# First tokens and weights in pieces, the first norm in halves, and idle matmuls ahead of the first product

## The chip, the cores and the metric

The kernel runs on one core of one Trainium2 chip. The metric is device time in microseconds (us) from one execution of the program; lower is better. Five engines work side by side, each with its own in-order instruction stream: TensorE (PE in the profile, with PEld for its weight loads), VectorE (DVE), ScalarE (ACT), GpSimd (POOL) and SyncE (SP), which issues all of this kernel's DMAs.

## The reference

There are 4 sequences of 1024 tokens with 1024 channels, all in float32. With `xn` the layernorm of the tokens over channels (no scale, no shift):

```
xn   = (x - mean) / sqrt(var + 1e-5)
ug   = xn * sigmoid(xn @ gate_w.T + gate_b)
aa   = tanh(a); um = mean over tokens of ug
d_eff = d + um @ d_lr_u @ d_lr_v / 4
s    = G * cumsum(b * ug / G),  G = cumprod(aa)       # per channel, over tokens
s    = c * s + d_eff * ug
h    = silu(silu(xn @ w1.T) @ w3.T) @ w2.T            # all tokens
top-2 routing: softmax(xn @ wr.T) -> expert numbers 0..7 and two gates
out_moe[expert number] += gate * h                    # rows 0..7 of the flat token axis alone
result = x + s * silu(out_moe)
```

An expert number is used as a row number, so only the first 8 rows of the result differ from `x`. All other work feeds those 8 rows: every token goes through the products with `w1` and `w3`, and every token of the first sequence through the gate product as well. Only the first 8 rows need `s`, so the recurrence is short.

## The kernel before

**Tiling.** Tokens are worked in four superblocks of 1024. The three big products are called `u` (tokens by `w1`), `g` (tokens by `gate_w`, superblock 0 alone) and `m` (the result of `u` by `w3`). Each is one Strassen-Winograd level over 2 x 2 blocks (seven block products instead of eight, names 1 to 7), and a block product is again divided into seven or, where it is called plain, eight small products. One small product is `small`, four `matmul` calls of 128x256 with two passes each, which makes the groups of eight matmuls that the profile shows. Operands are tokens with channels on the partitions (`xn[sb, I, J]`, token half I, channel half J) and weight blocks; sums and differences of blocks are made by DVE and POOL (`left_sums`, `t_sum`, `sub`).

**Order.** The order of the whole program is written out by hand. `at(place, f)` puts a piece of work at a place, a number on a scale in which one small product step of a block product is 2; `run_todo` runs what is due before each step. Every engine call goes through `Pinned`, which keeps the program order on each engine, and makes nearly every row of the profile carry line 89, so rows are told apart by tile names. `u` block 1 has steps at places 0, 2, 4, ... 14, and `g` block 1 at places 3, 5, ... 17. Both are plain, and both use the first token block `xn[0, 0, 0]`, with weight blocks `w1` (0, 0) and `gate_w` (0, 0). `u` block 2 starts at 16, `g` block 2 at 19 and `u` block 5 at 31. SP issues its DMAs in the same order; at most eight of them are outstanding in the head of the program.

**The head.** For superblock 0 the statistics are taken of tokens on the partitions. `load_x0` brings 256 tokens as two DMAs of 512 KB. `stats0` then does, on DVE, `bn_stats` twice for each 128 tokens (512 channels each) and a `bn_aggr`; it adds EPS, and ACT takes the square root; `scales` makes the reciprocal square root with one Newton step; four `tensor_scalar` calls turn the two means and the two scales into diagonal matrices (`dg`), and two `matmul` calls by a matrix of ones spread them over all partitions, in the PSUM tile `bc_00` (`acc` for the second 256 tokens, `bc_10` and `bc_11` for the others). `norm0` subtracts the mean and multiplies by the scale, on DVE, in place in the token block, each over 128 x 1024 elements. The transposed tokens `xT` come by DMAs of their own; the first block comes in two halves, the first half before and the second after the first weights.

**Weights.** `first_weights` loads the blocks of `w1` and of `gate_w`, each of 1 MB, and makes the Strassen sums from them. Those of `w1` are also written to DRAM for the other superblocks: `kept_sums_1` makes four sums of block 1 on POOL, and `keep_quarter` writes each of them back. POOL also makes the sums that the products need at once (`fresh_sums`, `left_sums`, and `five`, which is four subtractions for block 5).

Lines that matter here: `load_x0` 1007, `stats0` 236, `scales` 219, `norm0` 282, `first_weights` 508, `kept_sums_1` 524, the list of first loads and places 1031 to 1058.

Of the kernel before, what the change touches and what calls it, by code (L numbers as in the profile page):

```python
# [22 lines left out]
def kernel(  # L23
# [44 lines left out]
    NTOK, D = x.shape  # L68
# [6 lines left out]
    NT = SB // P  # L75
    EPS = 1e-5
    HB = ((0, 0), (0, 1), (1, 0), (1, 1))

    class Pinned:
# [27 lines left out]
    ps_sm = ctx.enter_context(tc.tile_pool(name="ps_sm", bufs=1, space=bass.MemoryType.PSUM))  # L107
# [3 lines left out]
    class Held:  # L111
# [11 lines left out]
                self.home.append(self.tile)  # L123

    NB, NQ = 20, 18
    blocks = deque(
        const.tile([P, 4, 2 * Q], F32, tag=f"b{i}", name=f"b{i}") for i in range(NB)
    )
# [4 lines left out]
    def block(uses=1):  # L133
        return Held(blocks, uses)

    def quarter(uses=1):
        return Held(quarters, uses)


    ident = const.tile([P, P], F32, tag="ident", name="ident")  # L140
    make_identity(nc, ident)
    ones = const.tile([P, P], F32, tag="ones", name="ones")
    pool.memset(ones, 1.0)

    sel = const.tile([P, E], F32, tag="sel", name="sel")

# [26 lines left out]
    def at(place, f, *args):  # L173

        seq[0] += 1
        heapq.heappush(todo, (place, seq[0], f, args))
# [25 lines left out]
    start = {}  # L202
# [13 lines left out]
        sync.dma_start(t.tile, xT[sb, I, J])  # L216
        xn[sb, I, J] = t

    def scales(v, w):

        sd = sp.tile([P, w], F32, tag=f"sd{w}", name="sd")
        act.activation(sd, v, AF.Sqrt)
        r0 = sp.tile([P, w], F32, tag=f"r{w}", name="r0")
        dve.reciprocal(r0, sd)
        e = sp.tile([P, w], F32, tag=f"e{w}", name="e")
        dve.tensor_mul(e, r0, r0)
        dve.tensor_mul(e, e, v)
        dve.tensor_scalar(e, e, -0.5, 1.5, ALU.mult, ALU.add)
        return r0, e

    def part(t, a):
        return t[:, 2 * a : 2 * a + 2, :].rearrange("p b (k n) -> p (b k) n", n=Q)
# [3 lines left out]
    def stats0(I, a, xb, lag):  # L236

        mv = sp.tile([P, 2, 2], F32, tag="mv", name=f"mv_{I}{a}")
        for tt in range(2):
            xt = xb[:, 2 * tt : 2 * tt + 2, :]  # L240
            bn = sp.tile([P, 2, nc.vector.BN_STATS_DIM], F32, tag=f"bn{tt}", name=f"bn_{I}{a}{tt}")
            for n in range(2):
                dve.bn_stats(bn[:, n, :], xt[:, n, :])
            dve.bn_aggr(mv[:, tt, :], bn)
        xb.drop()
        v = sp.tile([P, 2], F32, tag="v2", name=f"v_{I}{a}")
        dve.tensor_scalar(v, mv[:, :, 1], EPS, None, ALU.add)
        mean = mv[:, :, 0]
        dg = quarter()
        r0, e = scales(v, 2)  # L250
        dve.tensor_mul(e, e, r0)
        for s, w in ((0, mean), (1, e)):
            for tt in range(2):
                dve.tensor_scalar(
                    dg[:, (2 * s + tt) * P : (2 * s + tt + 1) * P],
                    ident,
                    w[:, tt : tt + 1],
                    None,
                    ALU.mult,
                )  # L260
        if (I, a) == (1, 1):
            bc = ps_sm.tile([P, 2, Q], F32, tag="sm", name="bc_11")
        elif (I, a) == (1, 0):
            bc = ps_y.tile([P, 2, Q], F32, tag="Y", name="bc_10")
        elif a == 1:
            bc = acc.rearrange("p (s n) -> p s n", s=2)
        else:
            bc = ps_acc.tile([P, 2, Q], F32, tag="rows", name="bc_00")
        yield lag
        for s in range(2):  # L270
            pe.matmul(
                bc[:, s, :],
                ones,
                dg[:, s * Q : (s + 1) * Q],
                start=True,
                stop=True,
                skip_group_check=True,
            )
        dg.drop()
        bc0[I, a] = bc  # L280

    def norm0(I, a, J):
        p = part(xn[0, I, J], a)
        bc = bc0[I, a]
        dve.tensor_tensor(p, p, bc[:, 0:1, :].to_broadcast([P, 4, Q]), ALU.subtract)
        dve.tensor_tensor(p, p, bc[:, 1:2, :].to_broadcast([P, 4, Q]), ALU.mult)

    def stats(sb, bcs):


        sums = sp.tile([P, NT], F32, tag="sums", name=f"sums_{sb}")
        sq = sp.tile([P, NT], F32, tag="sq", name=f"sq_{sb}")
        st = sp.tile([P, 2, NT], F32, tag="st", name=f"st_{sb}")
        for n in range(NT // 2):
            xb = block()
            row = sb * SB + n * 2 * P
            sync.dma_start(
                xb.tile.rearrange("p (t h) d -> p t (h d)", t=2),
                x[row : row + 2 * P, :].rearrange("(t p) d -> p t d", p=P),
            )  # L300
            at(here[0] + 5, squares, xb, 2 * n, sums, sq, st)
            yield 9 if sb == 1 else 6
        yield 9
        v = sp.tile([P, NT], F32, tag="v8", name=f"v_{sb}")
        dve.tensor_scalar(v, sq, 1.0 / D, EPS, ALU.mult, ALU.add)
        r0, e = scales(v, NT)
        dve.tensor_mul(st[:, 1, :], r0, e)
        ts = ps_sm.tile([2 * NT, P], F32, tag="sm", name=f"ts_{sb}")
        yield 5
        pe.transpose(ts, st.rearrange("p s t -> p (s t)"), ident)  # L310
        stT = sp.tile([2 * NT, P], F32, tag="stT", name=f"stT_{sb}")
        yield 1
        dve.tensor_copy(stT, ts)
        flat = dramp.tile([2 * NT, P], F32, tag=f"flat_{sb}", name=f"flat_{sb}")
        yield 0.5
        sync.dma_start(flat, stT)
        bcs[sb] = flat
# [124 lines left out]
    weights = {"w1": w1, "gw": gw, "w3": w3}  # L442
# [4 lines left out]
    T_OF = ((1, 0, None), (3, None, 0), (3, 1, None), (2, None, 1))  # L447
    T_AT = (1, 2, 4, 6)

    def load_w(name, KN, uses):  # L450
        t = block(uses)
        sync.dma_start(t.tile, weights[name][KN])
        return t

    def t_sum(o, t, s, j):
# [49 lines left out]
        sync.dma_start(o.tile, kept[{"u": "w1", "m": "w3"}[kind], i, j])  # L505
        op_ts[kind, sb, i, j] = o

    def first_weights(kind, name):

        keep = name == "w1"  # L510

        def S(i):
            return start[kind, 0, i]

        b = {}

        def load(key, KN, uses):
            b[key] = load_w(name, KN, uses)

        def one():  # L520

# [2 lines left out]
        def kept_sums_1():  # L524
            s = []
            for j in range(4):
                o = quarter(1 + (j < 2))
                t_sum(o, b[1], s, j)
                s.append(o)
                if j == 1:  # L530
                    s[0].drop()
                if j == 3:
                    s[1].drop()
                at(S(1) + 12 + 3 * j, keep_quarter, name, 1, j, o)
                yield 3
            b[1].drop()

# [33 lines left out]
            op_t[kind, 0, 3] = b[3]  # L571

        off = 0 if kind == "u" else 1
        load(1, (0, 0), 2 + keep)
        one()
        if keep:
            at(S(1) + 2, kept_sums_1)
        at(-20 + off, lambda: load(2, (1, 0), 2))
        at(-19, two)
        at(-12 + off, lambda: load(5, (0, 1), 3 + keep))  # L580
# [423 lines left out]

    x0 = {}

    def load_x0(I, a):
        xb = block()
        row = I * H + a * 2 * P
        for t in range(2):  # L1010
            sync.dma_start(
                xb[:, 2 * t : 2 * t + 2, :].rearrange("p h d -> p (h d)"),
                x[row + t * P : row + (t + 1) * P, :],
            )
        x0[I, a] = xb

# [11 lines left out]
    USES = {(0, 0): 4, (0, 1): 3, (1, 0): 3, (1, 1): 3}  # L1028
    G = {(0, 0): 2, (0, 1): 2, (1, 0): 1, (1, 1): 2}

    load_x0(0, 0)
    first = block(USES[0, 0] + G[0, 0])
    xn[0, 0, 0] = first
    sync.dma_start(first[:, 0:2, :], xT[0, 0, 0, :, 0:2, :])
    first_weights("u", "w1")
    load_x0(0, 1)
    sync.dma_start(first[:, 2:4, :], xT[0, 0, 0, :, 2:4, :])
    first_weights("g", "gw")
    at(-27, load_x0, 1, 0)
    at(-26, load_x0, 1, 1)  # L1040
    at(-25, load_xn, 0, 0, 1, USES[0, 1] + G[0, 1])
    at(-16, load_xn, 0, 1, 0, USES[1, 0] + G[1, 0])
    at(-15, load_xn, 0, 1, 1, USES[1, 1] + G[1, 1])
    at(-10, lambda: stats0(0, 0, x0[0, 0], 0))
    at(-9, norm0, 0, 0, 0)
    at(-8, lambda: stats0(0, 1, x0[0, 1], 11))
    at(-7, lambda: stats0(1, 0, x0[1, 0], 13))
    at(3.5, norm0, 0, 1, 0)
    at(3.6, lambda: stats0(1, 1, x0[1, 1], 6))
    at(4, norm0, 0, 0, 1)  # L1050
    at(5, norm0, 0, 1, 1)
    at(8, norm0, 1, 0, 0)
    at(9, norm0, 1, 0, 1)
    at(11, norm0, 1, 1, 0)
    at(12, norm0, 1, 1, 1)
    at(26, consts)
    for IJ in HB:
        at(0, lambda IJ=IJ: left.__setitem__(("u", 0, IJ), xn[(0,) + IJ]))
# [2 lines left out]
    for kind, sb, i, plain in line:  # L1061
        h = Half(kind, sb, i, plain)
        halves.append(h)
        S = start[kind, sb, i]
        n = 2 if sb == 0 and kind == "u" and i not in PLAIN_G else 1
# [13 lines left out]
    for sb in range(NS):  # L1079
        n = 2 if sb == 0 else 1  # L1080
# [78 lines left out]
    for n in range(2):  # L1159
        for k in range(2):  # L1160
            for g in range(4):
# [5 lines left out]
                    start=(k == 0),  # L1167
                    stop=(k == 1),
# [85 lines left out]
```

## Time and profile before

| what | value |
|---|---|
| time, median of 3 runs | 851.77 us (849.03 to 855.65) |
| the profiled execution's own time | 850.42 us |
| its span, first to last instruction | 848.7 us |
| mean granted TensorE clock | 0.997 |
| PE busy | 826.4 us, 97% of the span |
| DVE busy / POOL busy / ACT busy | 557.8 / 495.9 / 234.0 us |
| DMA moved | 189.71 MB |
| before 14.12 us: PE busy, DMA engines busy | 2.05 us, 88% |
| 14.12 to 834 us: PE busy | 815.4 of 819.9 us |
| 834 us to the end | 14.7 us, PE busy 9.0 |

In a row of the timeline the first number is the start in us from the first instruction, the second the time from the start of the group to its end; then engine, line, operation, output tile `<-` input tiles, shape and count. In brackets stands how long the engine had been idle before, and what ended the wait. Tiles `b` are the 20 blocks of 1 MB, `q` the 18 quarters of 256 KB; `b<-in_x` is a load of tokens, `b<-in_xT` of transposed tokens, `b<-in_w` of `w1` or `w3`, `b<-in_gw` of the gate weights. `X_u`, `Z_u`, `Y_u` are the PSUM tiles of the products with `w1`, `X_g` and `Z_g` those of the gate.

### The profile page before, as it was taken

The page shows a single profiled execution, that of the slowest core. Times are in us where ns is not written, and L with a number is a line of the kernel's source. Part 1 is how long each engine was busy: PE and PEld are TensorE (multiplying, and loading weights), DVE is VectorE, ACT ScalarE, POOL GpSimd, SP SyncE. Part 2 cuts the span into 40 slices and gives each one's busy share as a digit, 9 for nine tenths or more (in the row PEclk, how much of TensorE's full clock was granted, in tenths as well). Part 3 has the DMA queues.
Part 4 walks back from the last instruction along what each step waited for, and adds up shares of the span by engine and source line. Part 5 has one row for each costly group of instructions (what it writes and reads, how often), then busy time and mean ns, then how long its engine had stood idle before and what let it go on. Part 6 is the DMA issues. An engine that isn't in the chain of part 4 may idle for free.

```text
span 848.7 us, 11126 instructions
## 1 busy us (share of the span) xinstructions
PE 826.4 (97%) x4071; PEld 698.9 (82%) x4071; DVE 557.8 (66%) x894; ACT 234.0 (28%) x374; POOL 495.9 (58%) x374
## 2 busy tenths in 40 slices
PE   4999999989999999999999999999999999999997
PEld 3887888878888868888888778888888688888882
DVE  6959797987699425576797225775993246546642
ACT  0112213676121207343012226531122021220121
POOL 1479999994728764446865753753449444465400
PEclk9999999999999999999999999999999999999998
DMA  9944437721886876629867756649775455555600
GB/s 359 420 170 138 162 159 268 265 111 63 333 324 223 289 269 249 222 87 353 354 215 259 264 183 270 235 164 398 295 246 179 168 190 209 196 190 216 241 1 2
DMA packets 53181, 189.71 MB, mean 224 GB/s; under 512 B 6076, under 2 KB 9324, under 8 KB 41352
## 3 DMA queue, kind: packets, MB, share of 16 engines
q1 hardware_dynamic: 53128, 189.01, 60.5%
q8 instruction: 33, 0.54, 0.3%
q14 instruction: 20, 0.16, 0.1%
HBM read 165.86 MB, written 39.87 MB: 242 GB/s over the span
## 4 chain that ended last, share of the span: by engine, by line
PE 93%; DVE 5%; DMA 0%; issue 0%; ACT 0%; DVEq 0%; ACTq 0%
PE X_u L89 23%; PE X_m L89 22%; PE Z_m L89 12%; PE Z_u L89 11%; PE Y_u L89 5%; PE X_g L89 5%; PE Y_m L89 5%; DVE b L89 4%; PE Z_g L89 3%; PE acc L89 2%; PE plT L89 2%; PE Y_g L89 1%; PE pp L1163 1%; DMA b<-in_x 0%; PE bc L89 0%
## 5 line engine op out<-in xcount | busy, mean ns | idle before, releaser
L89 POOL TENSOR_TENSOR q<-b 128x512 f32<-128x512 f32 x144 | 202.2, 1416 | 231.2 <-DVE b L89 75.9
L89 ACT ACTIVATE b<-b 128x512 f32<-128x512 f32 (+1 forms) x152 | 105.0, 696 | 327.8 <-DVE b L89 318.8
L89 DVE TENSOR_TENSOR b<-b,b 128x512 f32<-128x512 f32 x176 | 177.8, 1030 | 3.0
L89 POOL TENSOR_TENSOR q<-b,q 128x512 f32<-128x512 f32 x91 | 133.1, 1465 | 5.7 <-issue 3.2
L89 POOL TENSOR_TENSOR b<-b,b 128x512 f32<-128x512 f32 x72 | 94.2, 1336 | 40.6 <-PE X_u L89 34.4
L89 DVE TENSOR_TENSOR b<-X_u,b 128x512 f32<-128x512 f32 x87 | 59.9, 689 | 75.5 <-PE X_u L89 74.7
L89 PE MATMUL X_u<-q,q 128*128 128x256 f32 x432 | 103.1, 382 | 1.0 <-DVE b L89 1.0
L89 PE MATMUL X_m<-q,q 128*128 128x256 f32 x416 | 98.3, 379 | 0.0
L89 DVE TENSOR_TENSOR b<-X_m,b 128x512 f32<-128x512 f32 x84 | 57.2, 686 | 62.0 <-PE X_m L89 60.7
L89 PEld LDWEIGHTS X_u<-q,q 128*128 128x128 f32 x432 | 81.3, 190 | 15.9 <-issue 2.6
L89 POOL TENSOR_TENSOR q<-q,b 128x512 f32<-128x512 f32 x53 | 72.0, 1359 | 30.3 <-PE X_u L89 26.2
L89 PEld LDWEIGHTS X_m<-q,q 128*128 128x128 f32 x416 | 79.1, 190 | 10.6
L89 DVE TENSOR_TENSOR b<-b,bc 128x1024 f32<-128x1024 f32 x60 | 72.5, 1212 | 4.3 <-ACT bc L89 2.3
L89 PE MATMUL X_u<-b,b 128*128 128x256 f32 x248 | 60.2, 388 | 5.2 <-DVE b L89 4.9
L89 PE MATMUL X_m<-b,b 128*128 128x256 f32 x272 | 63.8, 381 | 0.4 <-DVE b L89 0.4
L89 PEld LDWEIGHTS X_u<-b,b 128*128 128x128 f32 x248 | 48.0, 195 | 13.3 <-DVE b L89 6.1
L89 PEld LDWEIGHTS X_m<-b,b 128*128 128x128 f32 x272 | 51.5, 190 | 8.2 <-DVE b L89 1.4
L89 DVE TENSOR_TENSOR b<-Z_u,b 128x512 f32<-128x512 f32 x47 | 32.4, 688 | 31.3 <-PE Z_u L89 30.6
L89 PE MATMUL X_u<-b,q 128*128 128x256 f32 x216 | 51.4, 381 | 0.0
L89 PE MATMUL Z_u<-q,b 128*128 128x256 f32 x216 | 51.4, 381 | 0.0
L89 PE MATMUL Y_u<-b,b 128*128 128x256 f32 x216 | 51.3, 381 | 0.0
L89 PE MATMUL Z_u<-q,q 128*128 128x256 f32 x216 | 51.0, 379 | 0.0
(139 smaller groups left out, 1137.8 us busy)
## 6 DMA issues: line engine op xcount, KB each, us to landing
q<-w SPq DMA_DIRECT2D x160, 256.0 KB, 3.7
b<-in_w SPq DMA_DIRECT2D x36, 1024.0 KB, 7.7
b<-w_T SPq DMA_DIRECT2D x24, 1024.0 KB, 5.2
b<-in_xT SPq DMA_DIRECT2D x15, 1024.0 KB, 9.9
w<-q SPq DMA_DIRECT2D x56, 256.0 KB, 5.5
b<-in_x SPq DMA_DIRECT2D x12, 1024.0 KB, 7.3
w_T<-b SPq DMA_DIRECT2D x8, 1024.0 KB, 4.5
b<-in_gw SPq DMA_DIRECT2D x7, 1024.0 KB, 11.4
```

Source lines behind the costliest of these rows:

```text
L89: r = f(*args, **kwargs)
L1163: nc.tensor.matmul(pp[n][g * CG : (g + 1) * CG, :], accT[:, kk, :], w2_sb[n, kk // 4][:, kk % 4, :], start=(k == 0), stop=(k == 1),)
```

## The change

1. Sixteen `matmul` calls of ones by the identity, into a PSUM tile that nobody reads, stand first in PE's stream. A square root of one column stands first in ACT's.
2. The first 256 tokens come as four DMAs of 256 KB. The first half of the first transposed block comes as two DMAs of 256 KB, and the first block of `w1` as two of 512 KB (sub-blocks 0 and 2, then 1 and 3), taken in turns. The first gate weights now stand ahead of the second half of the first transposed block in SP's order.
3. In `stats0` ACT takes the square root straight from the variance, with EPS as its bias. The diagonals of the means are made ahead of the reciprocal, and after the reciprocal the Newton step takes three instructions, the last product folded in (it was four).
4. `norm0` of the first 256 tokens works in two channel halves: subtract and multiply the first, then the second.
5. Places move: the spreading of the second 256 tokens from 3 to 4.5 (after one more `u` step), of the third from 6 to 7, of the fourth from 9.6 to 12.2; the norms of superblock 0 to later places; `kept_sums_1` from 2 to 8 and its writes by 6.

```diff
     NB, NQ = 20, 18
+    IDLE = 16
...
+    eps = const.tile([P, 1], F32, tag="eps", name="eps")
+    pool.memset(eps, EPS)
+
+    root = const.tile([P, 1], F32, tag="root", name="root")
+    act.activation(root, eps, AF.Sqrt)
...
-    def scales(v, w):
-
-        sd = sp.tile([P, w], F32, tag=f"sd{w}", name="sd")
-        act.activation(sd, v, AF.Sqrt)
+    def scales(o, v, sd, w):
+
         r0 = sp.tile([P, w], F32, tag=f"r{w}", name="r0")
         dve.reciprocal(r0, sd)
         e = sp.tile([P, w], F32, tag=f"e{w}", name="e")
-        dve.tensor_mul(e, r0, r0)
+        dve.scalar_tensor_tensor(e, r0, -0.5, r0, ALU.mult, ALU.mult)
         dve.tensor_mul(e, e, v)
-        dve.tensor_scalar(e, e, -0.5, 1.5, ALU.mult, ALU.add)
-        return r0, e
+        dve.scalar_tensor_tensor(o, e, 1.5, r0, ALU.add, ALU.mult)
...
-        v = sp.tile([P, 2], F32, tag="v2", name=f"v_{I}{a}")
-        dve.tensor_scalar(v, mv[:, :, 1], EPS, None, ALU.add)
-        mean = mv[:, :, 0]
+        sd = sp.tile([P, 2], F32, tag="sd2", name=f"sd_{I}{a}")
+        act.activation(sd, mv[:, :, 1], AF.Sqrt, bias=eps)
         dg = quarter()
-        r0, e = scales(v, 2)
-        dve.tensor_mul(e, e, r0)
-        for s, w in ((0, mean), (1, e)):
+
+        def diagonals(s, w):
             for tt in range(2):
...
+        diagonals(0, mv[:, :, 0])
+        v = sp.tile([P, 2], F32, tag="v2", name=f"v_{I}{a}")
+        dve.tensor_scalar(v, mv[:, :, 1], EPS, None, ALU.add)
+        rs = sp.tile([P, 2], F32, tag="rs", name=f"rs_{I}{a}")
+        scales(rs, v, sd, 2)
+        diagonals(1, rs)
...
-    def norm0(I, a, J):
+    def norm0(I, a, J, parts=1):
         p = part(xn[0, I, J], a)
         bc = bc0[I, a]
-        dve.tensor_tensor(p, p, bc[:, 0:1, :].to_broadcast([P, 4, Q]), ALU.subtract)
-        dve.tensor_tensor(p, p, bc[:, 1:2, :].to_broadcast([P, 4, Q]), ALU.mult)
+        w = 4 // parts
+        for h in range(0, 4, w):
+            for s, op in ((0, ALU.subtract), (1, ALU.mult)):
+                row = bc[:, s : s + 1, :].to_broadcast([P, w, Q])
+                dve.tensor_tensor(p[:, h : h + w, :], p[:, h : h + w, :], row, op)
...
-    def load_w(name, KN, uses):
+    def load_w(name, KN, uses, before=()):
         t = block(uses)
-        sync.dma_start(t.tile, weights[name][KN])
+        if not before:
+            sync.dma_start(t.tile, weights[name][KN])
+        for b, f in enumerate(before):
+            f()
+            sync.dma_start(t[:, b::2, :], weights[name][KN][:, b::2, :])
         return t
...
-                at(S(1) + 12 + 3 * j, keep_quarter, name, 1, j, o)
+                at(S(1) + 18 + 3 * j, keep_quarter, name, 1, j, o)
...
-            at(S(1) + 2, kept_sums_1)
+            at(S(1) + 8, kept_sums_1)
...
-    def load_x0(I, a):
+    def load_x0(I, a, n=2):
         xb = block()
         row = I * H + a * 2 * P
-        for t in range(2):
+        w = 2 * D // n
+        for h in range(n):
+            t, c = h * w // D, h * w % D
             sync.dma_start(
-                xb[:, 2 * t : 2 * t + 2, :].rearrange("p h d -> p (h d)"),
-                x[row + t * P : row + (t + 1) * P, :],
+                xb.tile.rearrange("p h d -> p (h d)")[:, h * w : (h + 1) * w],
+                x[row + t * P : row + (t + 1) * P, c : c + w],
             )
...
-    load_x0(0, 0)
+
+    idle = ps_sm.tile([P, P], F32, tag="sm", name="idle")
+    for _ in range(IDLE):
+        pe.matmul(idle, ones, ident, start=True, stop=True, skip_group_check=True)
+    load_x0(0, 0, 4)
     first = block(USES[0, 0] + G[0, 0])
     xn[0, 0, 0] = first
-    sync.dma_start(first[:, 0:2, :], xT[0, 0, 0, :, 0:2, :])
-    first_weights("u", "w1")
+    first_weights(
+        "u",
+        "w1",
+        [
+            lambda b=b: sync.dma_start(first[:, b, :], xT[0, 0, 0, :, b, :])
+            for b in range(2)
+        ],
+    )
     load_x0(0, 1)
+    first_weights("g", "gw")
     sync.dma_start(first[:, 2:4, :], xT[0, 0, 0, :, 2:4, :])
-    first_weights("g", "gw")
...
-    at(-9, norm0, 0, 0, 0)
-    at(-8, lambda: stats0(0, 1, x0[0, 1], 11))
-    at(-7, lambda: stats0(1, 0, x0[1, 0], 13))
-    at(3.5, norm0, 0, 1, 0)
-    at(3.6, lambda: stats0(1, 1, x0[1, 1], 6))
-    at(4, norm0, 0, 0, 1)
+    at(-9, norm0, 0, 0, 0, 2)
+    at(-8, lambda: stats0(0, 1, x0[0, 1], 12.5))
+    at(-7, lambda: stats0(1, 0, x0[1, 0], 14))
+    at(4.6, norm0, 0, 1, 0)
+    at(4.7, lambda: stats0(1, 1, x0[1, 1], 7.5))
+    at(4.8, norm0, 0, 0, 1)
     at(5, norm0, 0, 1, 1)
     at(8, norm0, 1, 0, 0)
-    at(9, norm0, 1, 0, 1)
-    at(11, norm0, 1, 1, 0)
-    at(12, norm0, 1, 1, 1)
+    at(11, norm0, 1, 0, 1)
+    at(15, norm0, 1, 1, 0)
+    at(18, norm0, 1, 1, 1)
```

More of the change, by code (lines that the diff above doesn't have):

```diff
@@ L305, in stats @@
         dve.tensor_scalar(v, sq, 1.0 / D, EPS, ALU.mult, ALU.add)
-        r0, e = scales(v, NT)
-        dve.tensor_mul(st[:, 1, :], r0, e)
+        sd = sp.tile([P, NT], F32, tag="sd8", name=f"sd_{sb}")
+        act.activation(sd, v, AF.Sqrt)
+        scales(st[:, 1, :], v, sd, NT)
         ts = ps_sm.tile([2 * NT, P], F32, tag="sm", name=f"ts_{sb}")
@@ L506, in load_kept_sum, with first_weights @@
         op_ts[kind, sb, i, j] = o
-    def first_weights(kind, name):
+    def first_weights(kind, name, before=()):
         keep = name == "w1"
@@ L515, in first_weights, with load @@
         b = {}
-        def load(key, KN, uses):
-            b[key] = load_w(name, KN, uses)
+        def load(key, KN, uses, *before):
+            b[key] = load_w(name, KN, uses, *before)
         def one():
@@ L573, in first_weights @@
         off = 0 if kind == "u" else 1
-        load(1, (0, 0), 2 + keep)
+        load(1, (0, 0), 2 + keep, before)
         one()
         if keep:
-            at(S(1) + 2, kept_sums_1)
+            at(S(1) + 8, kept_sums_1)
         at(-20 + off, lambda: load(2, (1, 0), 2))
```

## The prediction

> **What bounds the kernel now.** I read the page first (shares, the chain of waits), then the timeline of the first 60 us, then the same head in stretches of 2 us.
>
> ```profile
> span 848.7 us, 11126 instructions
> PE 826.4 (97%) x4071; PEld 698.9 (82%) x4071; DVE 557.8 (66%) x894; ACT 234.0 (28%) x374; POOL 495.9 (58%) x374
> ...
> PE 93%; DVE 5%; DMA 0%; issue 0%; ACT 0%; DVEq 0%; ACTq 0%
> ```
>
> PE makes up 93% of the chain that ends last. From 14.12 to 834 us it is idle for only 4.5 us, so what this change can reach is the head, where PE stands still:
>
> ```profile
> 4.62 1.29 DVE L89 BATCH_NORM_STATS2 bn<-b 128x6 f32<-128x512 f32 x2 [2.61 <-DMA b<-in_x]
> 7.33 0.21 DVE L89 BATCH_NORM_AGGREGATE mv<-bn 128x2 f32<-128x12 f32 x1
> 8.02 0.17 DVE L89 RECIPROCAL r<-sd 128x2 f32<-128x2 f32 x1 [0.27 <-ACT sd L89]
> 9.28 0.48 DVE L89 TENSOR_SCALAR q<-ident,e 128x128 f32<-128x128 f32 x2
> 9.51 2.05 PE L89 MATMUL bc<-q,ones 128*128 128x256 f32 x4 [9.51 <-DVE q L89]
> 11.59 2.48 DVE L89 TENSOR_TENSOR b<-b,bc 128x1024 f32<-128x1024 f32 x2 [1.84 <-PE bc L89]
> 14.12 5.24 PE L89 MATMUL X_u<-b,b 128*128 128x256 f32 x16 [2.57 <-DVE b L89]
> 20.06 1.89 PE L89 MATMUL X_g<-b,b 128*128 128x256 f32 x8
> ```
>
> This is one serial chain: tokens land, statistics, a dozen small DVE steps, the spread, the norm, and the first product at 14.12 us. Behind it a second resource is full, the DMA engines (the two columns before the last number are granted clock and DMA share):
>
> ```profile
> 12.00:14.00 2.00, 0.00 (x0) 0.00 (x0) 1.97 (x3) 0.00 (x0) 0.76 (x1) 1.00 1.04 434
> 14.00:16.00 2.00, 1.88 (x5) 1.52 (x6) 1.97 (x6) 0.00 (x0) 0.00 (x0) 1.00 1.00 416
> 26.00:28.00 2.00, 2.00 (x11) 1.77 (x10) 1.97 (x4) 0.00 (x0) 1.46 (x2) 1.00 1.02 418
> ```
>
> A DMA share of about 1 at 416 GB/s means that loads land in the order of their bytes, whatever PE does: the head's loads are a fixed timetable against which an earlier PE may run.
>
> **The change, step by step**, in the time of the profiled execution (span 848.7, own time 850.42 us).
>
> *Tokens in four pieces.* The 1 MB had landed by 5.8 us (SP's wait on it). The pieces' last byte is no earlier, but VectorE needs only 0.64 us for each piece, so it now follows the loads: last `bn_stats` from about 6.0 to 6.7, aggregate until 6.9 instead of 7.54. Gain 0.6 us.
>
> *Statistics to diagonals.* From the end of the aggregate (7.54) to that of the last diagonal (9.76) took 2.22 us. ACT now starts at once (its 0.2 us lies beside the mean diagonals), and DVE issues two diagonals, the EPS sum, reciprocal, three small ones and two diagonals: eight starts at 0.2 us and a last diagonal of 0.28, 1.85 us. Ends at 8.75; gain 0.4 more.
>
> *Spread.* Four passes at 0.43 us stood in a row before (9.51 to 11.56, DVE at 11.59). The means' two go ahead under the small steps; the scales' two start at 8.85 and, at the warm 0.216 us a pass, DVE starts at 9.5. Gain here 1.1 us. If the clock is low it is 9.95.
>
> *Norm in halves.* A 128x1024 step took 1.24 us; the nearest 128x512 row of DVE with a PSUM operand is 0.69 (`b<-X_u,b`). First half done at 9.5 + 2 x 0.70 = 10.9, the second at 12.3. Products with `A[:, 0]` take eight passes, so they run until 12.65 and the second half is not waited for. DVE pays 0.3 us for the two extra instructions. Its block half and `w1`'s even sub-blocks, 1.75 MB into the stream, landed before 9 us even in the old order (all 2.5 MB had at 10.1, when POOL started on `w1`). **First product at 10.9 instead of 14.12.**
>
> *Idle matmuls.* The first product's weight loads tell the clock:
>
> ```profile
> 14.12 3.06 PEld L89 LDWEIGHTS X_u<-b,b 128*128 128x128 f32 x8 [3.29 <-DVE b L89]
> 17.25 1.70 PEld L89 LDWEIGHTS X_u<-b,b 128*128 128x128 f32 x8
> ```
>
> Eight passes took 3.13 us start to start, the next eight 1.73. Warm, the sixteen save 1.5 us. The idle calls, 32 passes of 128 columns, are not in the trace. Bounds: 0.108 us a pass (the `pl` transposes, 128x128, warm) and 0.43 (a cold 256-column pass); so 3.5 to 13.7 us from 1.6 on. I take half of the cold pass, 0.213, for half the columns: 6.8 us, ending by 8.5, just ahead of the scales' diagonals. At the upper end the spread waits until 15.3 and the change loses.
>
> The Trainium skill ("TensorE: Matmul & The Clock Gate", section "What's actually happening") says that a free-running window of about 3.4 us decides: one busy window releases the clock, one idle window takes it back. This trace agrees with the release (busy from 14.12, released at 17.25). The rule speaks against the change in one place: between 8.5 and 10.9 PE is idle for about 1.6 us, which falls short of an idle window, so by the rule the clock stays.
>
> *The gate weights end the gain.* Place 3 wants `gate_w`. In the old order it landed at 16.2 us: `w1` by 10, then 2.5 MB (tokens, half block, gate weights) at 0.415 MB/us. Put ahead of the half block (0.5 MB, 1.25 us) it would land at 15.0. Against that, 2.5 MB now travel in 2 KB rows: the trace's packets took 84 ns for 2 KB, 159 for 4 KB, 309 for 8 KB, hence 390, 412 and 424 GB/s, and 0.4 us more. So 15.4, while PE finishes the sixteen passes at 14.4 and stands for 1 us. Before, `X_g` began at 20.06 with 0.86 us of spreading (`acc`) ahead of it that now comes later: 19.2 against 15.45. **Gain 3.7 us**, and the warm clock is mostly swallowed by this wait.
>
> The Trainium skill ("DMA: Bandwidth & Descriptors", section "Measured (HBM→SBUF, 128 partitions, SWDGE, issued from GpSimd)") advises 1 MiB and more for each DMA. By its 2 us fixed cost, four more DMAs one after another would cost 8 us and make the change a loss. The row of DMA share (1.00 to 1.04 with eight in flight) says that fixed costs overlap here, so the sum holds none.
>
> *Does it persist?* Next come waits on DVE. `stats0` of the second tokens ends at about 16.8 (PE wants it at 18.9); the third's tokens land at 19.3, its diagonals are done at 22.8 (PE: 23.25); then `norm0` of the first block's second half, 2.46 us, ends at 25.3, and PE's fifth `u` step comes at 25.8. All fit, the last two by only 0.5 us. POOL's order takes two more sums (1.23 us each) ahead of block 5's subtractions, but its start on `left_sums` comes 2 us earlier with the norms; it ends its batch at about 56.4 and is next wanted at 61.94 - 3.7 = 58.2:
>
> ```profile
> 47.06 8.64 POOL L89 TENSOR_TENSOR b<-b,b 128x512 f32<-128x512 f32 x7
> 61.94 3.46 POOL L89 TENSOR_TENSOR q<-b 128x512 f32<-128x512 f32 x2 [6.24 <-DVE b L89]
> ```
>
> From there all is released by PE or DVE, and shifts. The moved writes of `w1` sums stand behind POOL in SP's queue, ahead of `consts`, which then issue at about 53 us and are wanted at 68: nothing. ACT's root hides under the table load before 2 us.
>
> **Sum.** 850.4 - 3.7 = 846.7 us. The median of the runs shown is 1.35 us above the profiled execution, so 848.0.
>
> **Rivals.**
> *Cold clock.* The release comes late or is lost in the gap. Then the spread ends 0.45 later and the sixteen passes take up to 1.5 more, 16.35 against the 15.45 of the gate weights: gain 2.8, 849.0. For it: the low clock at the old spread, with PE active in a third of the time. Against: 6.8 us of passes.
> *Late gate weights.* If small pieces slow the start (348 GB/s at 6 to 8 us already), they land at 16.3 as before: gain 2.8, 849.0.
> *Late norm.* DVE misses the fifth `u` step by 1 to 2 us: gain 2.2, 849.6. For it: margins of 0.5 us. Against: nothing in the rows.
> *POOL falls behind, and the kernel is slower.* Place: the batch of 17 sums and subtractions before 58 us. Beside DVE's SBUF work POOL's sums took 1.72 us (from 61.94), not 1.26. Price: 17 x 0.46 = 7.8 us, so it ends at 64.2, 6 us late; PE feeds directly from POOL's sums near 80 us (it waited there twice for 0.4 us), so all 6 arrive: 850.4 + 2.3, or 854.1 on the median's scale. It decides from 1.58 us a sum on. Against: beside norms with a PSUM operand, as here, POOL kept 1.27.
> *The idle calls do nothing:* that is the cold clock again.
>
> **Numbers.** Forecast 0.58, cold clock 0.14, late weights 0.10, late norm 0.10, POOL 0.08. The range takes in gains from 0.5 to 5 us and the scatter of the runs before (849.0 to 855.7): 844.5 to 853. Over or under 1% (8.5 us, about what a measurement of this kernel can tell from no change): PE's whole idle time in the head is 12 us, of which the chain leaves 9 to 10 in place, so faster by 1% has 0.04; slower by 1% needs POOL at twice its price or an idle burst at the upper end, 0.05.
>
> **What would show it.** After: `X_u` at about 10.9 with 0.216 us passes, `X_g` at about 15.4 after a wait of 1 us on a DMA, the fifth `u` step near 25.8 without a wait, PE busy without gaps until 150 us, span near 845. Wrong, if the first `bc` waits for PE, if `X_u` runs at 0.43 us a pass, if POOL's pause before 58 us is gone, or if a new wait opens behind 60 us.

## The result, and the profile after

The changed kernel takes 850.7 us (median of 22 runs, 848.07 to 852.09), the kernel before 850.91 (22 runs beside them, 849.03 to 855.65). The ratio is 0.9993 with a 95% interval of 0.9984 to 1.0002: no difference that this measurement can tell. The forecast was 848.0 in a range of 844.5 to 853, with 0.91 for a time within 1%. The time lies in the range and within 1%, but the range holds the unchanged time too, so that says little; the gain that was worked out, 3.7 us, is not there (0.2 between the medians). The forecast also stood 0.86 us too high on its own scale: the 1.35 us that it added came from three runs, and over 22 the median is 0.49 above the profiled execution. What follows is about the 3.5 us that are missing.

The page of the profiled execution after (own time 850.65 us, before 850.42): span, busy times, and the shares of the chain that ended last.

```profile
span 848.6 us, 11192 instructions
PE 831.2 (98%) x4103; PEld 701.9 (83%) x4103; DVE 565.7 (67%) x889; ACT 234.5 (28%) x375; POOL 496.6 (59%) x375
...
PE 87%; DVE 7%; DMA 4%; SPq 1%; issue 1%; ACT 0%; DVEq 0%; ACTq 0%
```

PE has 4.8 us more of busy time in the same span: the idle matmuls (6.42 us), less what the first passes save. The chain holds 4% of DMA where it held none. The head in the timeline of after:

```profile
1.60 6.42 PE L89 MATMUL idle<-ident,ones 128*128 128x128 f32 x32 [1.60 <-POOL eps L89]
...
7.47 0.69 DVE L89 BATCH_NORM_STATS2 bn<-b 128x6 f32<-128x512 f32 x1 [0.92 <-DMA b<-in_x]
...
8.20 0.21 DVE L89 BATCH_NORM_AGGREGATE mv<-bn 128x2 f32<-128x12 f32 x1
...
9.56 0.48 DVE L89 TENSOR_SCALAR q<-ident,rs 128x128 f32<-128x128 f32 x2
...
10.10 0.70 PE L89 MATMUL bc<-q,ones 128*128 128x256 f32 x2 [0.59 <-DVE q L89]
...
10.83 2.73 DVE L89 TENSOR_TENSOR b<-b,bc 128x512 f32<-128x512 f32 x4 [0.79 <-PE bc L89]
...
12.29 3.72 PE L89 MATMUL X_u<-b,b 128*128 128x256 f32 x16 [1.50 <-DVE b L89]
...
16.59 1.99 PE L89 MATMUL X_g<-b,b 128*128 128x256 f32 x8 [0.58 <-DMA b<-in_gw]
```

The bracket of the `bn_stats` row shows DVE waiting 0.92 us for the last of the four token pieces; the last aggregate now ends at 8.41 us (7.54 before). From there on everything is shorter, and the first product starts at 12.29 instead of 14.12, with 3.72 us for sixteen passes that took 5.24. Then `X_g` waits for the gate weights.

I call **lead** how much earlier a matmul starts in a kernel's profile than the same matmul in the profile before. After has a lead of 2.49 us from 20 to 67 us (up to 3.36 where a spreading that was moved back is still to come), 0.64 to 0.66 from 70 to 425 us, and 0.08 behind 431 us. So 1.85 us go at one place, at 67.6 us. The timeline of after around it:

```profile
50.81 8.61 POOL L89 TENSOR_TENSOR b<-b,b 128x512 f32<-128x512 f32 x7
...
54.63 5.94 DVE L89 TENSOR_TENSOR b<-b,b 128x512 f32<-128x512 f32 x2
...
62.45 3.46 POOL L89 TENSOR_TENSOR q<-b 128x512 f32<-128x512 f32 x2 [3.03 <-DVE b L89]
...
69.39 1.99 PE L89 MATMUL X_u<-b,b 128*128 128x256 f32 x8 [1.59 <-DVE b L89]
```

The same two sums of DVE, and the same product, in the timeline of the kernel before:

```profile
57.13 1.28 DVE L89 TENSOR_TENSOR b<-b,b 128x512 f32<-128x512 f32 x2
...
70.13 1.89 PE L89 MATMUL X_u<-b,b 128*128 128x256 f32 x8
```

These two are the first of the four sums (`s1`) that make the token block of `u` block 5; from here DVE works almost without a pause until PE's product at 69.39. Before, POOL's batch had ended (55.70) when they ran, and both took 1.28 us. After, the batch runs until 59.42, the first sum takes 5.34 us, until the batch is over, and the second 0.68. DVE is done 4.7 us later than with two sums of the usual length, POOL waits for it (3.03), and PE stands still ahead of `u` block 5: 1.97 us from one matmul's start to the next, where 0.22 is usual.

### The profile page after: what moved, and what is told of

It is laid out like the page before. It is cut to its first block, busy times and chain, and to the rows that moved or that the text cites. A ratio compares the mean times of both kernels' runs of the same rounds, so it can differ in the third digit from the quotient of the medians.

```text
span 848.6 us, 11192 instructions
## 1 busy us (share of the span) xinstructions
PE 831.2 (98%) x4103; PEld 701.9 (83%) x4103; DVE 565.7 (67%) x889; ACT 234.5 (28%) x375; POOL 496.6 (59%) x375
## 4 chain that ended last, share of the span: by engine, by line
PE 87%; DVE 7%; DMA 4%; SPq 1%; issue 1%; ACT 0%; DVEq 0%; ACTq 0%
PE X_u L89 21%; PE X_m L89 20%; PE Z_u L89 11%; PE Z_m L89 11%; DVE b L89 7%; PE Y_u L89 5%; PE X_g L89 5%; PE Y_m L89 4%; PE Z_g L89 3%; DMA b<-in_xT 3%; PE acc L89 2%; PE plT L89 2%; DMA b<-in_gw 1%; SPq L89 1%; PE Y_g L89 1%
## 5 line engine op out<-in xcount | busy, mean ns | idle before, releaser
L89 DVE TENSOR_TENSOR b<-b,b 128x512 f32<-128x512 f32 x176 | 181.8, 1052 | 3.3 <-POOL q L89 0.5
L89 DVE TENSOR_TENSOR b<-b,bc 128x1024 f32<-128x1024 f32 (+1 forms) x62 | 72.8, 1178 | 3.6 <-ACT bc L89 2.5
L89 DVE TENSOR_TENSOR b<-Z_m,b 128x512 f32<-128x512 f32 x48 | 32.8, 686 | 27.5 <-PE Z_m L89 26.1
```

The lines of the kernel that those rows point to most:

```text
L89: r = f(*args, **kwargs)
```

## The experiments

All ratios are to runs of the kernel before on the same chip (medians 851.03, 851.17 and 851.33 us in the three groups). There is one profile of each kernel, and a lead is that of the one profile: in five of them PE loses its clock near 171 us, which takes another 1.5 to 1.7 us of the lead (last section), and four lose 0.3 to 0.6 near 160 us.

**`sums_back`: the kept sums of block 1 at their old places.**

```diff
-                at(S(1) + 18 + 3 * j, keep_quarter, name, 1, j, o)
+                at(S(1) + 12 + 3 * j, keep_quarter, name, 1, j, o)
-            at(S(1) + 8, kept_sums_1)
+            at(S(1) + 2, kept_sums_1)
```

> The changed kernel, with the four kept sums of w1 block 1 put back at place 2 and their writes at 12, as in the kernel before; all else changed. Port theory (after the change, VectorE's first sum for u block 5 stands from 54.6 to 60.0 us because GpSimd's batch of sums, two sums longer by the move, holds a shared SBUF port until 59.4): the batch ends at about 57, the wait of 2.0 us ahead of u block 5 (at 69.4) goes to under 0.5, and the lead of PE over the kernel before at 100 us is 2.0 to 2.5 us instead of 0.64. Rival (VectorE is late by itself, through the norms at later places): the wait stays at 2.0 and the lead at 0.64. For the whole time: 848.5 us if the lead survives the loads at 380 to 410 us, 850.6 if these take it back.

Measured: 848.77 us, ratio 0.9969 (0.9958 to 0.9980). Its timeline:

```profile
48.70 8.63 POOL L89 TENSOR_TENSOR b<-b,b 128x512 f32<-128x512 f32 x7
...
55.04 3.44 DVE L89 TENSOR_TENSOR b<-b,b 128x512 f32<-128x512 f32 x2
...
60.36 3.45 POOL L89 TENSOR_TENSOR q<-b 128x512 f32<-128x512 f32 x2 [3.04 <-DVE b L89]
```

POOL's batch ends 2.1 us earlier, at 57.33. DVE's first sum takes 2.84 us, again until that end, and PE no longer waits ahead of `u` block 5: the lead is 2.09 us from 40 to 140 us. Two moved places are what cost the changed kernel most of its gain. (This profile is one of the five: it ends 0.86 us behind the one before. The ratio is of ten runs.)

**`whole_loads`: the first loads in the old sizes** (tokens 2 x 512 KB, the transposed half block 512 KB, `w1`'s first block 1 MB; the gate weights stay ahead of the second half block).

```diff
-    load_x0(0, 0, 4)
+    load_x0(0, 0)
...
-    first_weights("u", "w1", [lambda b=b: ... for b in range(2)])
+    sync.dma_start(first[:, 0:2, :], xT[0, 0, 0, :, 0:2, :])
+    first_weights("u", "w1")
```

> The changed kernel, with first tokens, first transposed half and first w1 block in the DMA sizes of the kernel before (two of 512 KB, one of 512 KB, one of 1 MB), gate weights still ahead of the second half block. Theory that the pieces of 2 KB rows start slowly (about 250 GB/s from 2 to 7 us against about 340): tokens land by 5.9 us instead of 7.45, the first product starts at about 10.9 instead of 12.3, gate weights land at 15.2 instead of 16.55, lead at 20 us about 3.6 instead of 2.5. Rival (the pieces are what lets the statistics start early): first product later than 12.3. At 100 us the port theory still allows only 0.6 to 1 us of lead, since GpSimd's batch ends near 59 us; without it the lead would be 3.6.

Measured: 849.97 us, 0.9988 (0.9975 to 1.0002). Its timeline:

```profile
5.63 1.23 DVE L89 BATCH_NORM_STATS2 bn<-b 128x6 f32<-128x512 f32 x2
...
11.00 3.72 PE L89 MATMUL X_u<-b,b 128*128 128x256 f32 x16 [1.50 <-DVE b L89]
...
15.90 1.99 PE L89 MATMUL X_g<-b,b 128*128 128x256 f32 x8 [1.18 <-DMA b<-in_gw]
...
53.94 6.11 DVE L89 TENSOR_TENSOR b<-b,b 128x512 f32<-128x512 f32 x2
```

The tokens had landed at 5.33 us (7.45 in pieces), the first product starts at 11.00, and the gate weights land at 15.86 instead of 16.55. Between these two profiles the pieces cost 1.3 us at the first product and 0.7 at `X_g`. Over all profiles less of this is left. The second aggregate ended at 7.72 to 8.41 us in the five profiles with pieces and at 7.07 to 7.54 in the eight without, so the pieces did come later. The warm first product started at 11.61 to 12.29 in those five and at 11.00 to 11.41 in four with whole loads and idle calls. But the gate weights, where they stand ahead of the half block, landed at 15.98 to 16.96 us with pieces and at 15.86 to 16.66 without: these overlap, and so do the ratios (0.9988 here against 0.9993 for the changed kernel; 0.9969 for `sums_back` against 0.9970 for `back_whole`). So the pieces gained nothing, and that they cost time at the end is not shown. The edit takes back three splits at once; that of `w1` need not be the bad one, since the whole block landed at about 11 us and the first product waited for it in `back_whole` and `g_later_gaps`. In this profile the lead is 3.19 us at 40 us; then DVE's long sum comes again (5.50 us), PE's wait takes 2.0, and 1.18 is left to the end.

**`back_whole`: both edits together.**

> Both together: kept sums of block 1 back at place 2, and the first loads whole. If both theories hold, the lead is 3.6 us at 20 us and 2.5 to 3.5 at 100 us, with no wait over 1 us ahead of u block 5. If the kept sums are not the cause, the lead at 100 us is that of whole loads alone. Whole time 847.5 us if nothing later takes the lead back, 850.5 if the loads at 380 to 410 us do.

Measured: 848.44 us, 0.9970 (0.9958 to 0.9982). Lead 2.81 us from 40 to 140 us and 2.47 to 2.69 to the end; DVE's first sum takes 2.73 us, and PE does not wait ahead of `u` block 5. In this profile PE lost its clock once in the head (11.35 to 14.76 us), so that the sixteen passes took 5.38 us and `X_g` followed at 16.38, 0.31 after the gate weights had landed (16.07): at this place the loss cost at most 0.3 us.

**`idle_only`: the kernel before, with the sixteen idle calls alone.**

```diff
+    idle = ps_sm.tile([P, P], F32, tag="sm", name="idle")
+    for _ in range(16):
+        pe.matmul(idle, ones, ident, start=True, stop=True, skip_group_check=True)
     load_x0(0, 0)
```

> The kernel before with the sixteen idle matmuls alone. If the clock is the cause of the slow first product: spread and first product at 0.216 us a pass, first product at about 13.6 instead of 14.12, its sixteen passes in 3.5 instead of 5.2 us, lead 2.0 at 20 us; with the kernel before's order of sums GpSimd's batch ends at 55.7, so 1.5 to 2 us of it stay at 100 us. Rival (the idle matmuls warm the clock, but it falls back before 13.6 us): lead 0 to 0.4. Whole time 849 if the lead lasts, 850.8 if the loads at 380 to 410 us take it back.

Measured: 851.51 us, 0.9996 (0.9983 to 1.0010). Its timeline:

```profile
8.95 1.13 PE L89 MATMUL bc<-q,ones 128*128 128x256 f32 x4 [0.62 <-DVE q L89]
...
12.65 3.72 PE L89 MATMUL X_u<-b,b 128*128 128x256 f32 x16 [2.57 <-DVE b L89]
...
32.38 1.10 PE L89 MATMUL bc<-q,ones 128*128 128x256 f32 x4 [0.85 <-DVE q L89]
```

The warm clock does what was forecast (four spreading passes 1.13 us instead of 2.05, the sixteen passes 3.72), which gives a lead of 1.64 to 1.72 us until PE comes to the spreading of the fourth tokens at its old place: there it waits for DVE, and 0.55 is left. So the later place of this spreading (9.6 to 12.2) probably carries part of what the changed kernel gains; no run moves it alone.

**`pool_sums`: the changed kernel with four sums on POOL that nobody reads, at place 23, behind its batch.**

```diff
+    def extra_sums():
+        t = xn[0, 0, 0]
+        for _ in range(4):
+            o = quarter()
+            pool.tensor_tensor(o.tile, t[:, 0], t[:, 1], ALU.add)
+            o.drop()
+
+    at(23, extra_sums)
```

> The changed kernel, with four sums on GpSimd that nobody reads (128x512, two operands in SBUF) added behind its batch of sums, ahead of u block 5. Port theory: VectorE's first sum for u block 5, which waited from 54.6 to 59.4 us for the batch to end, waits for these four as well, 4 x 1.23 = 4.9 us more; the wait of PE ahead of u block 5 grows from 2.0 to about 6.9 us, and the whole time to 854.5 to 855.6. Rival (VectorE is held up by something else, and GpSimd's work is only near it): the wait stays at about 2 us, the time at 850.7 to 851.5.

Measured: 855.38 us, 1.0046 (1.0032 to 1.0061). Its timeline:

```profile
51.54 7.41 POOL L89 TENSOR_TENSOR b<-b,b 128x512 f32<-128x512 f32 x6
54.87 10.13 DVE L89 TENSOR_TENSOR b<-b,b 128x512 f32<-128x512 f32 x2
...
58.90 4.94 POOL L89 TENSOR_TENSOR q<-b 128x512 f32<-128x512 f32 x4
...
65.65 3.27 PE L89 MATMUL X_u<-b,q 128*128 128x256 f32 x8 [2.80 <-DVE b L89]
```

DVE's first sum now takes 9.53 us: it stands through the rest of the batch and all four added sums, and the time is 4.7 us above the changed kernel's. PE's waits stand at two places (65.65 and 73.80), not at one, and PE lost its clock between them (66.21 to 69.63), so the 4.7 are not the price of the standing sum alone.

**`pool_memsets`: the same place, nine memsets of 128x512 on POOL instead.**

```diff
+    def extra_memsets():
+        for _ in range(9):
+            o = quarter()
+            pool.memset(o.tile, 0.0)
+            o.drop()
+
+    at(23, extra_memsets)
```

> The same with nine memsets of 128x512 on GpSimd in place of the four sums, about the same 4.5 us of GpSimd time (estimated from 0.31 us for a memset of 128x256), at the same place. If it is the SBUF reads of GpSimd's sums that hold VectorE, VectorE's sum starts at 59.4 us as in the changed kernel, the wait ahead of u block 5 stays at about 2 us, and only GpSimd's own next sums come up to 1.7 us later: 850.7 to 852. If any busy GpSimd holds it, the result is that of the four sums: about 855.

Measured: 850.18 us, 0.9976 (0.9962 to 0.9990). Its timeline:

```profile
51.53 8.77 POOL L89 TENSOR_TENSOR b<-b,b 128x512 f32<-128x512 f32 x6
...
54.06 3.43 DVE L89 TENSOR_TENSOR b<-b,b 128x512 f32<-128x512 f32 x2
...
60.24 4.25 POOL L89 MEMSET q<- 128x512 f32 x9
...
62.70 1.28 DVE L89 TENSOR_TENSOR b<-b,b 128x512 f32<-128x512 f32 x2
```

Beside memsets DVE's sums take 0.68 us each, as alone. But what I had expected of the place itself failed: the first sum did not stand through the batch. DVE and POOL took turns (1.75 and 1.71 us a sum), PE did not wait ahead of `u` block 5, and the lead stayed at 3.07 us until about 120 us (1.98 at 140). So the standing is not certain: here the same batch, with the memsets only behind it, let DVE in.

**`back_no_idle`: `back_whole` without the idle calls (`IDLE = 0`).**

> Kept sums back and first loads whole, without the idle matmuls. The spread and the sixteen first passes run at 0.43 us a pass for up to one window: first product at about 11.9 instead of 11.2, the gate's first product at 17.5 to 18.5 instead of 16.4, lead at 20 us 0.8 to 1.7 instead of 2.8. If the lead lasts as it does with them, the whole time is 849.5 to 850.5 against 848.4. If the clock is worth nothing here (as the wait for the gate weights hides it), 848.4.

Measured: 849.06 us, 0.9966 (0.9951 to 0.9981), not to be told from `back_whole`, though each interval is about 2.5 us wide and would hide the 1.36 us of lead between them. The first product runs at 0.43 us a pass and `X_g` starts at 17.74 instead of 16.38; the lead is 1.45 us from 40 to 160 us, against 2.81 until 140.

**`g_later`: `back_whole` with the gate's first block product two places later, and the third tokens' statistics behind the second norm.**

```diff
-        start[kind, sb, i] = END if kind != "g" else start["u", sb, i] + 3
+        start[kind, sb, i] = END if kind != "g" else start["u", sb, i] + (5 if i == 1 else 3)
...
-    at(-7, lambda: stats0(1, 0, x0[1, 0], 14))
     at(4.6, norm0, 0, 1, 0)
+    at(4.65, lambda: stats0(1, 0, x0[1, 0], 5.2))
...
-    at(8, norm0, 1, 0, 0)
+    at(10, norm0, 1, 0, 0)
```

> Kept sums back, first loads whole, and the gate's first block product starts at place 5 instead of 3 (behind the third step of u block 1, which needs no gate weights); the norm of the first block's second half comes ahead of the third tokens' statistics on VectorE, the spread of these goes to place 9.85 and the first norm with it to 10. Theory: the wait for the gate weights (1 us) is filled with work, the lead at 30 us is 3.5 to 4.5 instead of 2.8, and if VectorE's first sum for u block 5 still finds GpSimd's batch done in time, the whole time is 847 to 847.8. Rival: the lead runs into GpSimd's batch (ends at 56.5) and the wait ahead of u block 5 comes back: 848.4.

Measured: 847.39 us (6 runs, 846.28 to 848.35), 0.9945 (0.9925 to 0.9964), the lowest median of all. `Z_u` follows the sixteen passes without a wait for gate weights (16.47 in its timeline, `X_g` at 19.06). The lead is 2.72 us from 52 us and 1.85 at the end, in a profile that lost the clock in the head.

**`pool_gaps`: the changed kernel with a memset of 128x1 behind each sum of POOL's batch.**

```diff
                 t_sum(o, b[1], s, j)
+                pool.memset(gap, 0.0)
...
-            yield from sub(pool, b[5], b[5], b[1])
+            for _ in sub(pool, b[5], b[5], b[1]):
+                pool.memset(gap, 0.0)
+                yield 0.5
```

> The kernel after, with a memset of 128x1 on POOL behind each of the kept sums of w1's block 1 and behind each subtraction of both block 5, so that no two of POOL's sums of the batch follow each other directly. Theory (DVE's sum stands because POOL takes the next sum at once): DVE's first sum for u block 5 takes 0.7 to 1.8 us instead of 5.34, PE does not wait ahead of u block 5 (the 1.99 us from start to start there are gone), the lead on the kernel before stays 2.2 to 2.5 us at 100 us, and the time is 848.5 to 849. Rival 1 (DVE waits for the end of POOL's work list, whatever it holds): the sum again takes 5 us or more and ends at POOL's last sum, PE waits 2 us or a little more, 850.7 to 851.2. Rival 2 (the long sum was one event of that profile): the sum takes 1.75 us, but so it would in other executions of the kernel after; then the time does not differ from its median, 850.7.

Measured: 849.94 us, 0.9977 (0.9964 to 0.9989). Its timeline:

```profile
54.29 1.27 POOL L89 TENSOR_TENSOR b<-b,b 128x512 f32<-128x512 f32 x1
54.83 2.95 DVE L89 TENSOR_TENSOR b<-b,b 128x512 f32<-128x512 f32 x2
...
68.14 1.99 PE L89 MATMUL X_u<-b,b 128*128 128x256 f32 x8
```

POOL's batch ends later than in the changed kernel (60.59 against 59.42), and yet both sums of DVE are done in 2.95 us instead of 5.94, and PE starts `u` block 5 at 68.14 instead of 69.39, 0.31 us late instead of 1.75. So it was the standing sum, not POOL's late end, that PE waited for. The time is less good than the 848.5 to 849 expected: the lead is 1.9 us until 160 us, and in this profile PE lost its clock at 173.5 us, which took 1.59 of it.

**`g_later_gaps` and `g_later_no_idle`: `g_later` with the same memsets, and `g_later` without the idle calls.**

> The kernel with whole loads, the two places of block 1's kept sums back and the gate's first block two places later, with the same memsets on POOL. There the long sum of DVE (2.93 us) already cost PE nothing. If only PE's wait ahead of u block 5 counts, the time stays where it was, 847.4 (846.5 to 848.3). If the long sum also costs something later (the margin of DVE and POOL behind u block 5), it falls by up to 1 us, 846.5.

> The kernel with whole loads, the two places back and the gate's first block two places later, without the sixteen idle matmul calls. There nothing waits for the gate weights behind the first sixteen passes, so that a later or slower first product is paid in full. Theory (idle matmuls save time where no load ends the gain): four first spreading passes and the first product go slowly again, 1.3 us of the lead go, 848.7. Rival (DVE's chain of statistics and norms ends the gain by 30 us anyway): the lead behind 30 us is that of the kernel with idle matmuls, 847.4.

Measured: 847.91 us, 0.9955 (0.9939 to 0.9971) with the memsets, which add nothing where PE did not wait; 849.01 us, 0.9971 (0.9959 to 0.9984) without the idle calls. PE in the timeline of `g_later_gaps`:

```profile
11.41 3.69 PE L89 MATMUL X_u<-b,b 128*128 128x256 f32 x16 [1.85 <-DMA b<-in_w]
14.94 1.89 PE L89 MATMUL Z_u<-b,b 128*128 128x256 f32 x8
```

and in that of `g_later_no_idle`:

```profile
11.53 6.14 PE L89 MATMUL X_u<-b,b 128*128 128x256 f32 x16 [1.50 <-DVE b L89]
17.51 1.89 PE L89 MATMUL Z_u<-b,b 128*128 128x256 f32 x8
```

With nothing to wait for behind the first passes, the warm clock's 2.5 us reach the lead: 4.00 us against 1.68 from 52 to 160 us. All six runs of `g_later_gaps` lie below 848.3, ten of the twelve of `g_later_no_idle` above. I had expected 1.3 us of lead to go, and 2.3 went (2.0 at the end); the medians differ by 1.1.

## Why the prediction was right and wrong

**Right: that the gain is too small to tell.** Its first and largest reason was that only the head can move, and that held: the largest lead of any profile behind 52 us is 4.0 us.

**Statistics, spread, norm: right.** From the aggregate's end to the last diagonal's 1.63 us (forecast 1.85); from there to the first norm step 0.79 (0.75); norm of the first half 1.46 (1.4). With the old load sizes the first product starts at 11.00 (10.9), and at 11.17 to 11.41 in three more profiles.

**Idle matmuls: right in size, but the clock did not always stay.** 6.42 us until 8.02 (6.8 until 8.5), and the sixteen passes ran warm here. In three of the ten profiles with the idle calls (`back_whole`, `g_later`, `pool_sums`) the granted clock fell again at 11.35 to 11.60 us, for 3.41 us; the prediction took PE's pause before the first product to be too short for that, and there it was not. That the gate weights swallow part of the gain was right: in `back_whole` a cold first product costs at most 0.3 us at `X_g`, while without the idle calls `X_g` comes 1.36 us later (`back_no_idle`); moving the gate product away makes them worth 2.3 us of lead.

**Tokens in four pieces: wrong, in sign.** "The pieces' last byte is no earlier, but VectorE needs only 0.64 us for each piece" took for granted that it is no later. The pieces landed at 3.63, 5.03, 5.66 and 7.45 us. The aggregate ended at 8.41, not 6.9; before it was 7.54, and in no profile with pieces was it under 7.72. My sum held 0.4 us for all the small rows; at the aggregate the pieces came out 1.5 us (0.8 in the best profile) later than forecast. Whether that is the small rows or the later issue of the last piece (1.83 us for four issues, 0.88 for two) no run tells.

**Gate weights: a term too small.** Forecast to land at 15.4, they landed at 16.55, 0.17 later than before (16.38, where the prediction read 16.2) although they stand ahead of 0.5 MB. In the ten other profiles that have them ahead they land at 15.86 to 16.96, never at 15.4: on average at 16.46 with pieces and 16.18 without, so that the pieces explain about 0.3 of the 1.15 us and the rest is open. The gain at `X_g` was 2.5, not 3.7: this is the rival of late gate weights, which gave 2.8.

**All fit, by 0.5 us: right.** Neither the third tokens nor the fifth `u` step made PE wait; the lead is 2.49 us from 40 to 67 us.

**"From there all is released by PE or DVE, and shifts": the step that failed.** POOL's batch was to end at about 56.4. It ended at 59.42, because I let its start on `left_sums` come 2 us earlier, while it came later, at 38.48 instead of 37.21. In the timeline of before, and then of after:

```profile
30.82 0.16 DVE L89 TENSOR_TENSOR e<-r 128x2 f32<-128x2 f32 x1
...
37.21 1.27 POOL L89 TENSOR_TENSOR q<-b 128x512 f32<-128x512 f32 x1 [6.95 <-DVE b L89]
```

```profile
29.06 2.61 POOL L89 TENSOR_TENSOR q<-b 128x512 f32<-128x512 f32 x2 [27.23 <-DMA b<-in_w]
29.23 1.24 DVE L89 TENSOR_SCALAR v<-mv 128x2 f32<-128x2 f32 x1
...
30.58 1.12 DVE L89 SCALAR_TENSOR_TENSOR e<-r 128x2 f32<-128x2 f32 x1
...
31.73 1.19 DVE L89 TENSOR_TENSOR e<-e,v 128x2 f32<-128x2 f32 x1
...
38.48 1.27 POOL L89 TENSOR_TENSOR q<-b 128x512 f32<-128x512 f32 x1 [5.58 <-DVE b L89]
```

Two terms were wrong. DVE begins the fourth tokens only 0.52 us earlier than before (26.06 against 26.58). And their small steps now run beside POOL's sums: a step that takes 0.16 us alone takes 1.1 to 1.2, and from their last aggregate to the next norm 4.58 us pass instead of 2.77. The moved kept sums have no part in this: in `sums_back` the start is at 38.84. With that start and two more sums the batch is 3.7 us later than before, and only then does the failed step bite: I asked when POOL is next wanted (58.2), and not which DVE instruction would then run beside the batch. It was the first sum of `u` block 5, and it stood until the batch's end. The rival in which POOL falls behind had the place, but the wrong price: POOL's sums kept 1.23 to 1.27 us, and it was DVE that was held.

The Trainium skill ("SBUF — State Buffer", section "SBUF: two separate sides") says that a DVE operation with two SBUF inputs and a GpSimd operation that reads SBUF share one pair of ports, which the first to start keeps for its whole instruction. The runs agree on who is held (sums by sums, 1.75 us instead of 0.68; not by memsets, 0.68). They show more than it: the held sum may stand through two to eight of POOL's instructions.

**Sum.** 3.7 forecast; 1.2 lost at the gate weights, 1.85 to the standing sum: 0.65 is left, and the profile has 0.64 to 0.66 until 425 us. The last 0.57 go at about 430 us, at a wait whose length differs from profile to profile (0.5 to 1.6 us over the profiles, with and without the change), so I take it for scatter. 850.91 less 0.65 is 850.3, inside the measured interval, which no gain at all would be too.

**What stays open.** Why the sum stands through the batch in six profiles and takes turns in `pool_memsets`, whose batch has no gaps either, is not settled: POOL's sum had started 0.01 to 0.87 us ahead where it stood, and 0.07 where it took turns. How often the sum stands in the changed kernel itself is not known from its one profile. That a small memset between the sums lets DVE in was seen in two profiles.

## What to carry to other kernels

When work is moved on one engine, list what the other engine now runs beside it, not only when the moved work is next wanted: a 0.7 us DVE sum that fell beside a batch of POOL sums lasted, in six profiles, as long as the batch had left. Split a first load only if the trace shows that small pieces land no later; here the statistics that need the last of four pieces of 256 KB ended 0.2 to 1.3 us later than with two of 512 KB. A faster first product pays only if the next load behind it is not what PE waits for: put a product whose operands are there between them.

## What the runs showed of the hardware that I had not expected

**A held DVE instruction.** DVE's sum of two SBUF operands beside POOL's sums that follow each other without a pause took 2.73, 2.84, 2.93, 5.34, 5.50 and 9.53 us in six profiles, each time until the batch was over and then 0.7 us for the sum itself; elsewhere such sums alternate with POOL's at 1.7 to 1.8 us each.

**A wait of 2.7 us that sometimes costs 4.3.** Near 171 us every kernel here has a wait of PE of 2.74 to 2.76 us from start to start. In five of the thirteen profiles the granted clock then fell to half for 3.41 us, which took 1.5 to 1.7 us more. In `sums_back`, two stretches (busy times, granted clock, DMA share, GB/s):

```profile
170.35:173.76 3.41, 1.24 (x6) 0.76 (x4) 3.41 (x6) 2.54 (x4) 3.41 (x3) 1.00 0.41 171
173.76:177.17 3.41, 3.21 (x8) 2.58 (x9) 0.74 (x2) 3.21 (x6) 3.41 (x4) 0.50 0.75 291
```

and in after, on the same grid of 3.41 us counted from the release of its clock at 7.06 us:

```profile
170.87:174.29 3.42, 1.67 (x8) 1.14 (x6) 3.42 (x7) 2.97 (x4) 3.42 (x3) 1.00 0.28 115
```

With 1.24 us of PE work in the stretch the clock fell, with 1.67 it stayed: where the wait lies on the grid decides. The same count over every profile, each on its own grid, from the first release to 800 us: the nine stretches after which the clock fell hold 0.61 to 1.40 us of PE work, and every other one 1.43 us or more, so here the limit lies at about 41% of the stretch. It is not the whole rule: at the very end, near 833 us, stretches with 2.56 us of PE work, most of it products of 8 columns (`ta`), lost the clock too. The Trainium skill ("TensorE: Matmul & The Clock Gate", section "HAM oscillation — how this bites in real kernels") warns of gaps above about 3.4 us; here one of 2.7 us was enough, where it lay badly in the window.

**What scatters from run to run.** Of the 23 runs of the kernel before in the last group, eleven have a mean granted clock of 0.997 and a median of 850.47 us, ten 0.995 and 852.92. One more stretch of 3.41 us at half clock is just 0.002 of 850 us, but the 2.45 us between the medians are more than the 1.5 to 1.7 that such a stretch took in the profiles. At 0.997, `g_later` (3 runs) has 846.61, `g_later_gaps` (2) 846.57 and `g_later_no_idle` (10) 848.77: the 2.2 us between the last two agree with the 2.3 us of lead. That each of these differences is one lost window is worked out from the mean clock, not seen in a trace of every run.
